# Attention and a selective scan in one kernel: the end, where only the scan is left, with its sums on TensorE two scans later and its side jobs moved once per scan

## The chip, the cores and the metric

The kernel runs on one core of one Trainium2 chip. A core has five engines with a queue each: TensorE (PE in the profile, its weight loads PEld), VectorE (DVE), ScalarE (ACT), GpSimd (POOL) and SyncE (SP), which here issues nearly all transfers between memory and the chip's on-chip memory. The metric is the time of one execution on the device in microseconds; lower is better. The time shown is the median of three runs.

## The reference, cut to what matters

Layer 0 is attention over 4 images of 64 x 64 pixels, each 4096 tokens of 128 channels, with 4 heads, and a layer norm. Layer 1 adds three things that it computes from that: a 3 x 3 convolution, a mixing in the frequency domain, and a Mamba block. The Mamba block is what this change is about. Its core is a scan with 256 inner channels and 16 states for each:

```python
def step(h, inp):
    xt, dtt, Bt, Ct = inp
    dA = jnp.exp(dtt[..., None] * A)
    h = dA * h + dtt[..., None] * Bt[:, None, :] * xt[..., None]
    y = jnp.einsum('bdn,bn->bd', h, Ct)
    return (h, y)
...
return ys.transpose(1, 0, 2) + x * D
...
y = y * jax.nn.silu(z)
return jnp.einsum('bld,od->blo', y, out_proj_w)
```

So for each of the 16 states there is a decay dA, an input term dt·B·x, a recurrence along the tokens, and a product with C; the 16 products and x·D are summed, multiplied by the gate silu(z), and projected.

## The kernel before, in words

The 4 x 4096 tokens are cut into 32 chunks of 512 (eight to an image). 128 channels lie on the 128 partitions, and the 512 tokens of a chunk along a row. The 256 inner channels are two halves.

The order of all work is written out by hand as a loop over steps `t` (the loop at the end of the function). Attention takes one step per block of 128 keys for one pair of heads and one chunk of queries: 64 steps a chunk, up to step 2048. In each step TensorE computes scores twice (L450 for the row maxima, L490 for the exponentials), VectorE takes maxima (L457), ScalarE takes exponentials (L498), and TensorE multiplies with the values (L510).

The scan runs beside it, 144 steps later, so that it goes on for 2.2 chunks after attention has ended, up to step 2190. One scan (one state of one half) is two steps; a chunk has 32 scans. At an odd step the next scan is prepared: `scan_decay` puts dA into a bank of PSUM with ScalarE (L823), `scan_input_term` forms the input term `db` (L828, GpSimd during attention, VectorE after it), and `scan_load` brings the rows of B and C, spread over all partitions, with a DMA from SP's queue (L806, or L812 for one that goes into memory that the keys and values of attention have left). At an even step `scan_state` runs the recurrence on VectorE (L839), copies the last value of the state (L848) and multiplies with C on GpSimd (L849), and adds the product to the sum. Which engine adds depends on the chunk: up to chunk 29 GpSimd (L866 the first time, with x·D, and L868), for the chunks 30 and 31 TensorE, which multiplies with the identity and sums in PSUM (L861, L862). In these two chunks the scan's result `hs` goes into one of four tiles that held values of attention (`VA[v % 4]`, V in the profile), otherwise into one of two buffers.

Everything else of layer 1 and the small steps of attention are jobs: Python generators that `Plan.step` moves on. A job yields a string of what its next stretch needs: P, D or A for a place on TensorE, VectorE or ScalarE, B for a bank of PSUM (there are two), x and f for buffers, or nothing. `Plan.step` sorts the jobs by rank and gives each whose need is met one stretch, and goes on at once with a job only if it needs P alone. How many places there are is told at each step. After attention it is called at every step, that is twice per scan, with four places for each of the three engines:

```python
if t < -LEAD or t > HALVES * NT:
    plan.step(t, {"D": 4, "P": 4, "A": 4})
```

The instructions of a step are put in the engines' queues in the order in which the program issues them, and each queue is worked off in that order. Within one odd step the decay, the input term and the load come first, then the jobs; within an even step the scan, its product and its sum come first.

The jobs that still run after attention are: `normalise` (the last one: L537 to L554, with four small DMAs and VectorE's reciprocal L545) and `output_projection` (L569 to L606) of chunk 31, `mamba_input` (L648 to L669), `scan_input` (L683 to L708), with the sigmoid (L622 to L632: Abs, Exp, Ln on ScalarE, a difference on VectorE, Exp), `scan_bc` (L720 to L730), `scan_dt` (L738 to L770) and `spectral` (L878 to L900) of chunk 31; `convolve` (L913 to L923) and `gate` (L779 to L787) of the chunks 30 and 31; `scan_output` (L934 to L985) of the chunks 29 to 31, which multiplies the sums with the gates (L957 or L960), projects them (L970), adds (L976, L943, L944) and stores; and the four `flips` of the last image. `scan_output` of a chunk is due two steps after the chunk's 64 steps of scanning.

Of the kernel before, what the change touches and what calls it, by code (L numbers as in the profile page):

```python
# [9 lines left out]
F32 = mybir.dt.float32  # L10
F32R = mybir.dt.float32r
AF = mybir.ActivationFunctionType
ALU = mybir.AluOpType
# [4 lines left out]
P = 128  # L18
# [5 lines left out]
L = 512  # L24
# [3 lines left out]
NH = DI // P  # L28
NS = 16
# [54 lines left out]
class Job:  # L84
# [17 lines left out]
class Plan:  # L102


    def __init__(self, banks, buffers):
        self.t = None
        self.places = buffers
        self.seq = 0
        self.later = []
        self.jobs = []  # L110
        self.free = list(range(banks))
        self.freed = []
# [11 lines left out]
    def step(self, t, places):  # L124

        self.t = t
        self.places |= places
        self.free += [bank for when, bank in self.freed if when <= t]
        self.freed = [e for e in self.freed if e[0] > t]
        for e in sorted((e for e in self.later if e[0] <= t), key=lambda e: e[:3]):  # L130
            self.jobs.append((e[1], e[0], e[2], Job(e[3])))
            self.later.remove(e)
        self.jobs = sorted((j for j in self.jobs if not j[3].done), key=lambda j: j[:3])
        kept = 0
        for *_, job in self.jobs:
            bank = None
            if "B" in job.need and len(self.free) <= kept:
                continue
            if any(c != "B" and not self.places[c] for c in job.need):
                kept += "B" in job.need  # L140
                continue
            for c in job.need:
                if c == "B":
                    bank = self.free.pop(0)
                else:
                    self.places[c] -= 1
            job.advance(bank)
            while not job.done and job.need == "P" and self.places["P"]:
                self.places["P"] -= 1
                job.advance(None)  # L150
        self.jobs = [j for j in self.jobs if not j[3].done]

# [5 lines left out]
def attention_then_conv_mamba(  # L158
# [17 lines left out]
    nc = tc.nc  # L176
# [3 lines left out]
    NT = N // P  # L180
    CHUNKS = B * NCH
    HALVES = CHUNKS * PAIRS
# [19 lines left out]
    for h in range(HEADS):  # L202
        k, j = divmod(h, 2)
        c = COL["bk"] + k
# [8 lines left out]
    for h in range(HEADS):  # L213
        k, j = divmod(h, 2)
        c = COL["bq"] + h
# [38 lines left out]
    ident = cst[:, K_ID : K_ID + P]  # L254
# [68 lines left out]
    plan = Plan(2, {"x": 2, "f": 1})  # L323
# [311 lines left out]
    xps, xss, dts, us, accs, gates, xds, bcds = ({} for _ in range(8))  # L635
# [194 lines left out]
    def scan_state(c, v):  # L830

        n, hf = divmod(v, NH)
        k = hf * NS + n
        assert (c, hf) in scaled
        if c >= CHUNKS - 2:
            hs = flat(VA[v % 4])
        else:
            hs = loc.tile([P, L], F32, tag="hs", name=f"hs_{c}_{k}")
        nc.vector.tensor_tensor_scan(  # L839
            hs,  # L840
            dA.pop((c, v)),
            db.pop((c, v)),
            state[:, k : k + 1] if c % NCH else zero,
            ALU.mult,
            ALU.add,
        )
        if c % NCH < NCH - 1:
            nc.gpsimd.tensor_copy(state[:, k : k + 1], hs[:, L - 1 :])  # L848
        nc.gpsimd.tensor_tensor(hs, hs, bcs[c, n][1], ALU.mult)  # L849
        if hf == NH - 1 and (c, n) in taken:  # L850
            spare.append((plan.t + 6, taken.pop((c, n))))
        elif hf == NH - 1:
            ring[0] += 1
        if c >= CHUNKS - 2:

            if v == 0:
                late = psum.tile([P, NH, L], F32, tag=f"s{CHUNKS - c}", name=f"acc_{c}")
                for h in range(NH):
                    accs[c, h] = late[:, h, :]
            if n == 0:  # L860
                nc.tensor.matmul(accs[c, hf], ident, xss[c][hf], start=True, stop=False)  # L861
            nc.tensor.matmul(accs[c, hf], ident, hs, start=False, stop=n == NS - 1)  # L862
        elif n == 0:
            acc = loc.tile([P, L], F32, tag=f"acc{hf}", name=f"acc_{c}_{hf}")
            accs[c, hf] = acc
            nc.gpsimd.tensor_tensor(acc, xss[c][hf], hs, ALU.add)  # L866
        else:
            nc.gpsimd.tensor_tensor(accs[c, hf], accs[c, hf], hs, ALU.add)  # L868

    hxs, yms, edges, wd, ymd = {}, {}, set(), {}, {}  # L870

# [74 lines left out]
    def scan_output(c):  # L946

        b, i = divmod(c, NCH)
        late = i < NCH // 2
        yield "f"  # L950
        while not all(gates[c]) or c not in yms:
            yield ""

        for hf in range(NH):
            if c >= CHUNKS - 2:
                acc = loc.tile([P, L], F32, tag=f"acc{hf}", name=f"acc_{c}_{hf}")
                nc.vector.tensor_tensor(acc, accs[c, hf], gates[c][hf], ALU.mult)  # L957
                accs[c, hf] = acc
            else:
                nc.gpsimd.tensor_tensor(accs[c, hf], accs[c, hf], gates[c][hf], ALU.mult)  # L960
        if not late:
            wr = load_flipped(c)
        for _ in range(3):
            yield ""
        bank = yield "PB"
        pf = bank_tile(bank, [P, L], f"py1_{c}")
        for hf in range(NH):
            if hf:
                yield "P"
            nc.tensor.matmul(  # L970
                pf, outw[:, hf, :], accs[c, hf], start=hf == 0, stop=hf == NH - 1
            )
        yield "D"
        plan.release(bank, 2)
        ob = loc.tile([P, L], F32, tag="ob", name=f"ob_{c}", bufs=1)
        nc.vector.tensor_tensor(ob, yms.pop(c), pf, ALU.add)  # L976
        if late:
            yield ""
            ymd[c] = dram.tile([P, L], F32, tag="ymd", name=f"ymd_{c}", bufs=NCH)
            nc.sync.dma_start(ymd[c], ob)  # L980
        else:
            add_flipped(ob, wr)
            yield ""
            yield ""
            nc.sync.dma_start(out[b, :, i * L : (i + 1) * L], ob)  # L985
        plan.places["f"] += 1
# [20 lines left out]
    LEAD = 7  # L1007
    SLOT = PAIRS * NT
    LAG = 2 * SLOT + 16
# [19 lines left out]
    for c in range(CHUNKS):  # L1029
        t0 = (c + 1) * SLOT  # L1030
        plan.at(t0, 0, load_residual(c))
        plan.at(t0 + 16, 1, mamba_input(c))
        plan.at(t0 + SLOT + 30, 3, convolve(c))
        plan.at(c * SLOT + LAG + 6, 3, gate(c))
        plan.at((c + 1) * SLOT + LAG + 2, 0, scan_output(c))
    for b in range(B):
        for i in range(NCH // 2):
            plan.at((b + 1) * NCH * SLOT + 44 + 10 * i, 4, flips(b * NCH + NCH // 2 - 1 - i))
# [1 line left out]
    t = 6 - SLOT  # L1040
    loaded = 0
    end = (CHUNKS + 3) * SLOT
    while t < end or not plan.idle():
        H, m = divmod(t, NT)
        if 0 <= H < HALVES:
            scores_for_exp(H, m)
        h1, s1 = divmod(t + LEAD, NT)
        if 0 <= h1 + 1 < HALVES:
            scores_for_max(h1 + 1, s1)
        H, m = divmod(t - 1, NT)  # L1050
        last = m == NT - 1
        if last and 0 <= H < HALVES:
            times_values(H, m)
        c, s = divmod(t - LAG, SLOT)
        odd = s % 2 == 1
        if -1 <= c < CHUNKS:
            v = c * STATES + s // 2
            if not odd:
                if v >= 0:
                    scan_state(*divmod(v, STATES))  # L1060
            else:
                if 0 <= v + 1 < CHUNKS * STATES:
                    scan_decay(*divmod(v + 1, STATES))
                if 0 <= v + 2 < CHUNKS * STATES:
                    late = t > HALVES * NT
                    scan_input_term(
                        *divmod(v + 2, STATES), nc.vector if late else nc.gpsimd
                    )

                if loaded < CHUNKS * NS and loaded // NS in bcds:  # L1070
                    if ring[0] or spare[0][0] <= t:
                        scan_load(*divmod(loaded, NS))
                        loaded += 1
        if t < -LEAD or t > HALVES * NT:
            plan.step(t, {"D": 4, "P": 4, "A": 4})
        elif odd:
            plan.step(t, {"D": 2, "P": 2, "A": 2})
        else:
            plan.step(t, {"D": 0, "P": 0, "A": 1})
        if not last and 0 <= H < HALVES:  # L1080
            times_values(H, m)
        t += 1
# [76 lines left out]
```

## Time and profile before

| what | value |
| --- | --- |
| median of three runs | 6060.06 us (6060.05 to 6060.12) |
| the profiled execution's own time | 6062.53 us |
| its span | 6060.8 us |
| TensorE busy | 5849.3 us, 97% |
| VectorE busy | 4360.3 us, 72% |
| ScalarE busy | 3585.5 us, 59% |
| GpSimd busy | 4488.8 us, 74% |
| last instruction of attention's values ends, scan 12 of chunk 29 begins | 5820 us |
| first scan of chunk 30 begins | 5851.66 us |
| first scan of chunk 31 begins | 5970.70 us |
| last scan ends | 6050.2 us |

The profile is one execution, and its times count from the start of its span. A row of a timeline gives start, duration, engine, line, operation and operands (out<-in), and in brackets how long the engine had been idle just before and what ended that. A row of waits names the waiting engine and line, whom it waited for, the total in us, the number of times and the longest. A row of the windows gives for a stretch of the span the busy time of each engine with the number of its instructions, then TensorE's granted clock as a share of full speed, the DMA engines' share and GB/s. A float32 matmul stands there as two records.

Two names differ in the profile from the text: the tiles V and K are also what the scan uses after attention, for its states and for B and C. A busy TensorE row is modelled at its end, so it is not TensorE at its best.

### The profile page before, as it was taken

The numbers are of one execution on the slowest core, as the hardware profiler recorded it, in microseconds if no ns is written. First come the engines' busy times: TensorE is split into PE (matmuls) and PEld (weight loads), VectorE is DVE, ScalarE is ACT, GpSimd is POOL, SyncE is SP. The second block draws the span as 40 slices with busy tenths as digits, with TensorE's granted clock in tenths as the row PEclk, the third lists the DMA queues.
The fourth block names the chain that finished last, engine by engine and source line by source line (L and its number), as shares of the span: only waits on it lengthen the run. The fifth ranks groups of instructions, "written<-read, shape, count | busy, mean of one in ns | idle before, by whom it ended". The sixth has DMA issues, their size and how long they took to land. (4 is left out here: it accounts for less than half of the span.)

```text
span 6060.8 us, 82716 instructions
## 1 busy us (share of the span) xinstructions
PE 5849.3 (97%) x31370; PEld 2443.2 (40%) x31370; DVE 4360.3 (72%) x4565; ACT 3585.5 (59%) x4826; POOL 4488.8 (74%) x4530
## 2 busy tenths in 40 slices
PE   5999999999999999999999999999999999999966
PEld 2444444444444444444444444444444444444322
DVE  4557777777777777777777777777777777777647
ACT  1455666666666666666666666666666666666643
POOL 0006888778887777888887888877888887788877
PEclk7999999999999999999999999999999999999988
DMA  4012222224333322223432222222433222222233
GB/s 124 25 36 58 66 72 75 69 73 109 86 84 76 73 67 74 76 64 87 105 89 78 73 66 71 75 71 70 110 81 84 70 69 64 66 67 63 71 86 84
DMA packets 266641, 455.28 MB, mean 75 GB/s; under 512 B 46688, under 2 KB 48256, under 8 KB 266240
## 3 DMA queue, kind: packets, MB, share of 16 engines
q1 hardware_dynamic: 261584, 448.11, 28.3%
q8 instruction: 246, 4.03, 0.3%
q10 hardware_dynamic: 4656, 1.87, 0.1%
q14 instruction: 155, 1.27, 0.1%
HBM read 375.68 MB, written 65.80 MB: 73 GB/s over the span
## 5 line engine op out<-in xcount | busy, mean ns | idle before, releaser
L457 DVE TENSOR_REDUCE part<-s 128x2 f32<-128x1024 f32 x2048 | 2499.2, 1221 | 1413.1 <-PE s L450 1409.3
L498 ACT ACTIVATE e<-s 128x1024 f32<-128x1024 f32 x2048 | 2095.6, 1023 | 2121.3 <-PE s L490 2116.7
L510 PE MATMUL po<-e,V 128*33 128x512 f32 x8192 | 2180.9, 605 | 2.4 <-DVE oz L521 0.3
L490 PE MATMUL s<-Q,K 64*128 64x512 f32 x8192 | 1500.6, 444 | 13.5 <-ACT e L498 10.2
L450 PE MATMUL s<-K,Q 64*128 64x512 f32 x8192 | 1314.7, 399 | 38.0 <-DVE part L457 28.9
L849 POOL TENSOR_TENSOR hs<-hs,bc 128x512 f32<-128x512 f32 x952 | 1215.9, 1277 | 170.7 <-DVE hs L839 101.4
L490 PEld LDWEIGHTS s<-Q,K 64*128 64x128 f32 x8192 | 610.2, 184 | 1736.3 <-ACT e L498 1237.8
L828 POOL TENSOR_TENSOR db<-u,bc 128x512 f32<-128x512 f32 x948 | 1215.9, 1283 | 0.0
L868 POOL TENSOR_TENSOR acc<-acc,hs 128x512 f32<-128x512 f32 x900 | 1154.7, 1283 | 70.6
L839 DVE TENSOR_TENSOR_SCAN hs<-dA,state,db 128x512 f32<-128x512 f32 x832 | 1060.6, 1275 | 52.6 <-ACT dA L823 37.9
L450 PEld LDWEIGHTS s<-K,Q 64*128 64x128 f32 x8192 | 752.9, 186 | 295.3 <-DVE part L457 128.1
L490 PE MATMUL s<-MX,sel 64*128 64x512 f32 x4096 | 808.3, 391 | 0.0
L823 ACT ACTIVATE dA<-dt,negA 128x512 f32<-128x512 f32 x1024 | 703.4, 687 | 113.4 <-DVE V L839 54.7
L848 POOL COPY state<-hs 128x1 f32<-128x1 f32 x864 | 159.0, 184 | 789.4 <-DVE hs L839 785.7
L510 PEld LDWEIGHTS po<-e,V 128*33 128x33 f32 x8192 | 305.3, 109 | 886.6 <-issue 840.9
L490 PEld LDWEIGHTS s<-MX,sel 64*128 64x128 f32 x4096 | 383.5, 185 | 90.8
L913 PE MATMUL pf<-xp,cw 128*128 128x512 f32 x576 | 287.9, 618 | 0.0
L554 POOL TENSOR_TENSOR op<-op,rz 128x512 f32<-128x512 f32 x32 | 40.9, 1278 | 178.5 <-DMA rz<-rd 175.6
L839 DVE TENSOR_TENSOR_SCAN hs<-dA,zero,db 128x512 f32<-128x512 f32 x128 | 163.2, 1275 | 1.0 <-POOL db L828 0.7
L862 PE MATMUL acc<-V,cst 128*128 128x512 f32 x128 | 89.1, 798 | 74.3 <-POOL V L849 74.0
L913 PEld LDWEIGHTS pf<-xp,cw 128*128 128x128 f32 x576 | 96.6, 188 | 118.5 <-issue 117.0
L708 POOL TENSOR_TENSOR xs<-xs,sg_x 128x512 f32<-128x512 f32 x64 | 82.3, 1286 | 76.5 <-ACT sg_x L632 76.5
(146 smaller groups left out, 3555.2 us busy)
## 6 DMA issues: line engine op xcount, KB each, us to landing
bc<-bcd SPq DMA_DIRECT2D x487, 512.0 KB
Q<-qd SPq DMA_DIRECT2D x256, 128.0 KB
K<-kd SPq DMA_DIRECT2D x64, 256.0 KB
K<-bcd SPq DMA_DIRECT2D x42, 256.0 KB
vd<-vst SPq DMA_DIRECT2D x32, 264.0 KB
V<-vd SPq DMA_DIRECT2D x32, 264.0 KB
xq<-in_x SPq DMA_DIRECT2D x32, 256.0 KB
xk<-in_x SPq DMA_DIRECT2D x32, 256.0 KB
```

The source lines that it names most:

```text
L450: nc.tensor.matmul(sc[:, j, :], QT[H][rows[j], n, t * P : (t + 1) * P], KK[k][m][rows[j], :], start=n == 0, stop=n == 1,)
L457: nc.vector.tensor_reduce(part[H][:, t, :, m], sc, AX.X, ALU.max)
L490: nc.tensor.matmul(s[:, j, :], sel[rows[j], :] if n == 2 else KK[k][i][rows[j], t * P : (t + 1) * P], mov[rows[j], :], start=n == 0, stop= ...
L498: nc.scalar.activation(e, s, AF.Exp)
L510: nc.tensor.matmul(po[H][used[j], :], VA[i][:, t, 2 * k + j, :], e[:, j, :], start=m == 0, stop=m == NT - 1,)
L823: nc.scalar.activation(dA[c, v], dts[c][hf], AF.Exp, scale=negA[:, k : k + 1])
L828: engine.tensor_tensor(db[c, v], us[c][hf], bcs[c, n][0], ALU.mult)
L839: nc.vector.tensor_tensor_scan(hs, dA.pop((c, v)), db.pop((c, v)), state[:, k : k + 1] if c % NCH else zero, ALU.mult, ALU.add,)
L848: nc.gpsimd.tensor_copy(state[:, k : k + 1], hs[:, L - 1 :])
L849: nc.gpsimd.tensor_tensor(hs, hs, bcs[c, n][1], ALU.mult)
L868: nc.gpsimd.tensor_tensor(accs[c, hf], accs[c, hf], hs, ALU.add)
L913: nc.tensor.matmul(pf, cw[:, k, :], xps[c][:, dy : dy + RPC, dx : dx + W], start=k == 0, stop=False)
```

## The change

There are four parts, all of them for the steps after attention.

1. `late` in `scan_state` no longer goes by the chunk (30 and 31) but by the step, so that the last six scans of chunk 29 also write into the four V tiles and are summed by TensorE.
2. The sums are not issued with the product. They are put on a list with a due step four later, and `add_states`, called at each step after attention's end ahead of the jobs, issues those that are due. Four steps are two scans.
3. Jobs are moved on only at odd steps, once per scan, with four places for VectorE and TensorE and six for ScalarE, and a job goes on within the step as long as it needs one place of P, A or D alone and there is one.
4. Chunk 29 has two partial sums for each half, GpSimd's and TensorE's. Its output joins them with an addition on VectorE and multiplies with the gate there too, as chunks 30 and 31 did before. The output of the chunks 29, 30 and 31 is due six steps after the chunk's 64 steps instead of two.

The bank for TensorE's sum is named by the chunk's parity, and the loop guards against an empty list of spare places. The diff, cut:

```diff
-            while not job.done and job.need == "P" and self.places["P"]:
-                self.places["P"] -= 1
+
+            while not job.done and job.need in ("PAD" if self.late else "P"):
+                if not job.need or not self.places[job.need]:
+                    break
+                self.places[job.need] -= 1
                 job.advance(None)
...
-        if c >= CHUNKS - 2:
+        late = plan.t > HALVES * NT + 1
+        if late:
             hs = flat(VA[v % 4])
...
-        if c >= CHUNKS - 2:
-
-            if v == 0:
-                late = psum.tile([P, NH, L], F32, tag=f"s{CHUNKS - c}", name=f"acc_{c}")
-                for h in range(NH):
-                    accs[c, h] = late[:, h, :]
-            if n == 0:
-                nc.tensor.matmul(accs[c, hf], ident, xss[c][hf], start=True, stop=False)
-            nc.tensor.matmul(accs[c, hf], ident, hs, start=False, stop=n == NS - 1)
+        if late:
+
+            if c not in sums_late:
+                sums_late[c] = psum.tile(
+                    [P, NH, L], F32, tag=f"s{1 + c % 2}", name=f"acc_{c}"
+                )
+            terms = [hs] if n else [xss[c][hf], hs]
+            for x in terms:
+                waiting.append((plan.t + 4, c, hf, x, n == NS - 1 and x is hs))
...
+    def add_states():
+        while waiting and waiting[0][0] <= plan.t:
+            _, c, hf, x, last = waiting.pop(0)
+            nc.tensor.matmul(
+                sums_late[c][:, hf, :], ident, x, start=(c, hf) not in begun, stop=last
+            )
+            begun.add((c, hf))
...
-            if c >= CHUNKS - 2:
-                acc = loc.tile([P, L], F32, tag=f"acc{hf}", name=f"acc_{c}_{hf}")
-                nc.vector.tensor_tensor(acc, accs[c, hf], gates[c][hf], ALU.mult)
-                accs[c, hf] = acc
+            if c in sums_late:
+                total = sums_late[c][:, hf, :]
+                if (c, hf) in accs:
+                    nc.vector.tensor_tensor(accs[c, hf], accs[c, hf], total, ALU.add)
+                    total = accs[c, hf]
+                else:
+                    accs[c, hf] = loc.tile([P, L], F32, tag=f"acc{hf}", name=f"acc_{c}_{hf}")
+                nc.vector.tensor_tensor(accs[c, hf], total, gates[c][hf], ALU.mult)
...
-        plan.at((c + 1) * SLOT + LAG + 2, 0, scan_output(c))
+        plan.at((c + 1) * SLOT + LAG + (2 if c < CHUNKS - 3 else 6), 0, scan_output(c))
...
-        if t < -LEAD or t > HALVES * NT:
+        plan.late = t > HALVES * NT
+        if plan.late:
+            add_states()
+            if odd:
+                plan.step(t, {"D": 4, "P": 4, "A": 6})
+            plan.t = t
+        elif t < -LEAD:
             plan.step(t, {"D": 4, "P": 4, "A": 4})
```

In the built program this leaves every engine's order as it was up to the end of attention, and after it GpSimd has eight instructions fewer, VectorE four more, and SP the same transfers, some of them in another order.

More of the change, by code (lines that the diff above doesn't have):

```diff
@@ L106, in __init__ @@
         self.t = None
+        self.late = False
         self.places = buffers
@@ L868, in scan_state @@
             nc.gpsimd.tensor_tensor(accs[c, hf], accs[c, hf], hs, ALU.add)
+    sums_late, waiting, begun = {}, [], set()
+    def add_states():
[5 more added lines that the diff above has]
+            begun.add((c, hf))
     hxs, yms, edges, wd, ymd = {}, {}, set(), {}, {}
@@ L1070, in attention_then_conv_mamba @@
                 if loaded < CHUNKS * NS and loaded // NS in bcds:
-                    if ring[0] or spare[0][0] <= t:
+                    if ring[0] or spare and spare[0][0] <= t:
                         scan_load(*divmod(loaded, NS))
                         loaded += 1
-        if t < -LEAD or t > HALVES * NT:
+        plan.late = t > HALVES * NT
[5 more added lines that the diff above has]
+        elif t < -LEAD:
             plan.step(t, {"D": 4, "P": 4, "A": 4})
```

## The prediction

> **What bounds the kernel now.** I read the 40 slices first: TensorE is at 9 tenths to the 38th slice and falls to 6 after it, so almost the whole span is attention and only the end is anything else. In the built order no instruction of any engine moves before the end of attention, so 5820 us of the 6060.8 us span cannot change. Next I cut the rest by chunk of the scan with the windows table. The last eight scans of chunk 29 run to 5852, chunk 30 to 5971, chunk 31 to 6050, and then comes the end of the last output.
>
> ```profile
> core 0: us, PE busy (x) PEld busy (x) DVE busy (x) ACT busy (x) POOL busy (x), PEclk, DMA share, GB/s
> 5820.00:5852.00 32.00, 6.25 (x12) 2.04 (x10) 20.97 (x31) 9.30 (x16) 28.66 (x29) 0.60 0.20 54
> 5852.00:5971.00 119.00, 72.48 (x118) 26.53 (x118) 82.28 (x85) 45.91 (x80) 79.25 (x91) 0.72 0.50 139
> 5971.00:6050.00 79.00, 52.74 (x96) 17.25 (x94) 63.89 (x67) 26.72 (x41) 58.83 (x39) 0.91 0.20 47
> 6050.00:6061.00 11.00, 4.33 (x9) 1.27 (x8) 2.17 (x4) 0.00 (x0) 3.01 (x4) 0.90 0.06 24
> ```
>
> Only the first stretch has a nearly full engine (POOL, 28.66 of 32.00). In the other two nobody is full, and VectorE, which carries every scan, is idle for 36.7 and 15.1 us. With 11.0 in the first stretch that is 62.8 us of idle VectorE; nothing longer can be won there. The rows without side jobs show what a scan costs when nothing disturbs it: 1.92 us from scan to scan, 1.28 for the scan and the rest for its input term.
>
> ```profile
> 6034.29 1.28 DVE L839 TENSOR_TENSOR_SCAN V<-dA,state,db 128x512 f32<-128x512 f32 x1
> 6035.60 0.69 DVE L828 TENSOR_TENSOR db<-u,K 128x512 f32<-128x512 f32 x1
> 6036.22 1.28 DVE L839 TENSOR_TENSOR_SCAN V<-dA,state,db 128x512 f32<-128x512 f32 x1
> ```
>
> Then the waits from 5820 on: who waited, for whom, us in total, times, longest.
>
> ```profile
> PE acc L862 <- POOL V L849: 74.0, 39, 6.1
> DVE V L839 <- ACT dA L823: 19.6, 8, 5.4
> DVE ob L976 <- PE py L970: 12.5, 3, 6.9
> DVE hs L839 <- POOL acc L868: 10.6, 5, 4.0
> DVE sg_z L630 <- ACT ln_z L627: 6.9, 1, 6.9
> DVE conv L693 <- ACT xi L688: 4.2, 1, 4.2
> ```
>
> TensorE, hardly loaded, sits 74 us waiting for GpSimd's product, because the sum of a state is put in its queue right after the state's product was issued. Whatever a side job asks of TensorE stands behind that wait. The timeline shows the longest case.
>
> ```profile
> 5862.74 1.26 POOL L849 TENSOR_TENSOR V<-V,bc 128x512 f32<-128x512 f32 x1
> ...
> 5864.06 0.45 PEld L862 LDWEIGHTS acc<-V,cst 128*128 128x128 f32 x2 [3.38 <-POOL V L849]
> ...
> 5867.57 1.88 PE L970 MATMUL py<-acc,outw 128*128 128x512 f32 x4
> ...
> 5869.49 0.69 DVE L976 TENSOR_TENSOR ob<-ym,py 128x512 f32<-128x512 f32 x1 [6.87 <-PE py L970]
> 5870.10 1.28 DVE L839 TENSOR_TENSOR_SCAN V<-dA,state,db 128x512 f32<-128x512 f32 x1
> ```
>
> GpSimd's products let the sums go at 5864.06, the output product follows them, and VectorE, whose next instruction needs it, starts the next scan at 5870.10 after 6.87 us of nothing.
>
> **What the Trainium skill says.** *TensorE: Matmul & The Clock Gate*, "Architectural detail", says that ScalarE's, VectorE's and GpSimd's queues are strict FIFOs, while TensorE can pull weight loads ahead; the stall just shown agrees for matmuls and VectorE. The same page, "What's actually happening", says that TensorE runs at half rate after an idle window of about 3.4 us and at full rate after a busy one: the trace agrees, one state's sum takes 1.12 us in dense stretches and 2.08 us after long waits. *SBUF — State Buffer*, "Who interferes with whom", says that a VectorE tensor_tensor with both inputs in SBUF and a GpSimd instruction exclude each other; agreed, the input term takes 0.69 us alone and up to 1.79 us here.
>
> **The change, part by part.**
> *Sums two scans later.* In chunks 30 and 31 these idle stretches before VectorE's instructions lead back to TensorE behind a product: 6.87 (py), 4.20 (pi), 2.11 (p1), 3.35 (pw), 2.58 (pd) in chunk 30, 4.05 (py) and 3.31 (pz) in chunk 31, together 26.5 us. Two scans later (3.8 us) the product, 1.27 us, is usually done, and TensorE goes through. What is late next is ScalarE's chain of the job, below. A tile is written again four scans later, so a sum has two scans to spare.
> *Chunk 29's last states.* Six sums leave GpSimd (6 x 1.44 = 8.7 us) and two gate products (2 x 1.49 = 3.0). VectorE gets four instructions, two joins and two gates, 0.65 each as L957's pair in 1.29: 2.6 us, in chunk 30's stretch and in VectorE's own sequence, so paid. TensorE gets six sums of at most 2.08 us where it is busy 6.25 of 32 us: nothing, unless it is late for the fifth scan. The scans no longer wait for two hs buffers: 10.6 us of idle go. Two things come in their place. The load of the reciprocals' input (L542) now stands in SP's queue behind the load of chunk 30's first B and C, which waits for a product that ended at 5831.7; before it was issued at 5822.39. It lands some 4 us after 5832.2 (rd to rz took 4.1), and VectorE's reciprocal stands ahead of scan 14, so VectorE stops at about 31.4 and goes on at 36: 4.6 us. Then rd and rz (4.1 and some 3) bring GpSimd's L554 to 43.7, the projection (2.07) to 47.1, and VectorE, ready at 43.9, waits 3.3 us at L572 ahead of chunk 30's first scan. 10.6 go, 7.9 come, and the L630 that stands earlier costs nothing new: about 3.5 us won with the small gaps.
> *Jobs once per scan, chains in one step.* A sigmoid now puts Abs and Exp into one step and Ln into the next: 0.62 + 0.62 + dA 0.69 + Ln 0.68 is 2.6 us, up to 3.9 with the copy 0.60 and two edge copies, while VectorE has one scan and one input term, 1.92, before it meets L630. So each leaves 1 to 2 us: 2.1, 1.8 and 1.4 in chunk 30 (the first hides behind join and layer norm), 1.8 twice in chunk 31. The projection pd stands behind four taps of the convolution (0.88 each, 16 records in 7.03) and a sum: 1.8. The convolution's result ym stands ahead of the next decay on ScalarE: six taps and a sum, 6.2 us, less 2.7 of VectorE's work: 3.7 in chunk 30. In chunk 31 ten taps and two sums, 10.6, less 7: 4. The dt chain of the first half ahead of decay 9: 1.8. GpSimd gets both halves' L761 to L763 (2 x 4.6) and a flip (1.9) close together, scans then outrun the four tiles: 4 and another 2. Loads for the flips now have two scans to land instead of one; I keep 2 us for the one at the start of chunk 31.
> *Sum of what stays.* Chunk 30: 2.1 + 1.8 + 1.4 + 1.8 + 3.7 + 1.8 + 6 = 18.6; the terms' waits for GpSimd, which are inside the 82.28 us of busy time, cover part of it, I take 16. Its length: 82.3 + 2.6 + 16 = 101 instead of 119, won 18. Chunk 31: 63.9 + 3.6 + 4 + 2 and 1.5 for the outputs' products = 75 instead of 79, won 4. The end keeps its 11 us, as its order is the same. In all 3.5 + 18 + 4 = 25.5 us. The profiled execution took 6062.53 with a span of 6060.8; the runs' median 6060.06 is 0.7 below the span. 6060.8 - 25.5 - 0.7 = 6034.6, so **6035**.
> *Bounds.* The residual waits are the unknown, no row shows them. Nothing less than none: 62.8 - 2.6 = 60 us won, 6000. At the other end all 62.8 come back in new places, with 2.6 us more: 6063, and more only by the last rival.
>
> **Rivals.**
> *VectorE is nearly full.* For it: TensorE, ScalarE and GpSimd have 46, 73 and 40 us to spare in chunk 30. Against it: the chains above have only one scan to hide in. With a third of my 35 us of residual waits (7.9 + 16 + 11), 23 more are won: 6012.
> *Products more than two scans late.* GpSimd is busy 79.25 of 119 us, and without the two gates 76 in 101 is 75%; if bursts keep it two scans behind for most of chunk 30, TensorE blocks as before and that chunk keeps its idle time. Then 3.5 + 4 are won: 6053, no change as measured.
> *ScalarE's answer in VectorE's queue, slower.* Seven sigmoids (one in chunk 29, four in 30, two in 31) have L630 ahead of a scan. If ScalarE starts each only after a half-rate input product (2.1) behind two half-rate sums (4.2), the wait is 2.6 + 6.3 = 8.9 each without cover: 62 us, with 7.7 for the two ym, 7.9 in chunk 29 and 2.6 new work 80 against 62.8 won: 6078. It costs more than is won from 6.4 us per sigmoid. Against it: only one of the seven showed as much before (6.9).
> *It does not do what it says:* excluded, the built order has the sums two scans later.
>
> **How the numbers follow.** Forecast, 6022 to 6047: 0.62. VectorE nearly full, 6000 to 6022: 0.17. Late products, 6048 to 6072: 0.14. Slower: 0.07. A measurement of this kernel tells about 0.2%, 12 us, from no change, so faster is 0.79, same 0.14, slower 0.07. The range 6012 to 6053 leaves out half of the second and third case and the last.
>
> **What would show it.** The same rows: TensorE waiting for the product well under 74 us; L976 after py, L693 after xi near nothing; the hs wait gone and a wait of VectorE at the reciprocal and at L572; new waits of the sigmoid's difference for Ln of 1 to 2 us; ym ahead of a decay still 3 to 4. Chunk lengths near 28, 101 and 75. I am wrong if chunk 30 stays above 110, if attention's part moves, or if VectorE's input terms slow far beyond their 0.9 us.

## The result and the profile after

The changed kernel takes 6039.84 us (median of 7 runs, 6038.33 to 6043.57) where the kernel before takes 6060.05 (7 runs beside it): ratio 0.9968, 95% interval 0.9957 to 0.998, 20.2 us less. The profiled execution took 6038.33 with a span of 6036.5. The lines have moved: the scan is L844 (before L839), its product L854 (L849), the sum on TensorE L880 (L862), the decay L827 (L823), the sigmoid's difference L634 (L630) after Ln L631 (L627), the addition to the projection L995 (L976), the reciprocal L549 (L545), the attention projection's result L576 (L572).

The windows table of the kernel after, cut as that of before (the columns are the same: PE, PEld, DVE, ACT, POOL busy, then clock, DMA share, GB/s):

```profile
5818.00:5846.00 28.00, 8.99 (x14) 2.73 (x13) 19.01 (x21) 9.77 (x15) 23.64 (x24) 0.68 0.28 63
5846.00:5953.00 107.00, 70.73 (x126) 25.51 (x125) 84.20 (x98) 46.33 (x80) 76.61 (x87) 0.74 0.51 153
5953.00:6026.00 73.00, 53.69 (x97) 17.80 (x95) 64.69 (x68) 26.90 (x41) 60.45 (x39) 0.90 0.19 51
6026.00:6037.00 11.00, 4.24 (x8) 1.27 (x8) 2.00 (x4) 0.00 (x0) 2.84 (x4) 0.97 0.07 25
```

VectorE's busy column hardly changes; it is the lengths that shrink. Measured from scan to scan in the timeline (from the first scan after attention, eight scans before the end of chunk 29, to the first scan of chunk 30, from there to the first scan of chunk 31, and on to the end of the last scan), the three stretches of time took 30.8, 119.0 and 79.5 us before and 27.5, 106.9 and 73.0 after. So 3.3 + 12.1 + 6.5 = 21.9 us were won there. Attention ended 2.2 us earlier in this execution, and the end stayed (10.6 before, 10.5 after). VectorE's idle time in the windows fell from 11.0 + 36.7 + 15.1 to 9.0 + 22.8 + 8.3 us.

The waits of VectorE after the end of attention, and from the whole list of waits the row of TensorE:

```profile
PE acc L880 <- POOL V L854: 63.5, 38, 14.9
```

```profile
DVE V L844 <- ACT dA L827: 10.4, 3, 5.1
DVE V L844 <- PE acc L880: 8.3, 2, 5.0
DVE oz L525 <- ACT oz L524: 7.3, 1, 7.3
DVE zc L549 <- DMA zc<-zd: 6.3, 1, 6.3
DVE dtr L731 <- ACT dtr L730: 3.7, 1, 3.7
DVE sg_x L634 <- ACT ln_x L631: 2.8, 2, 1.5
```

TensorE still waits for products, but less than the 63.5 suggests: 14.9 of it is the first sum of chunk 29, in a stretch where it holds up nobody. What matters is who stands behind. `hs` waiting for GpSimd (10.6 before) and `conv` waiting for `xi` (4.2) are gone from the list, `ob` waiting for `py` fell from 12.5 to 2.5. What is left are answers of ScalarE (dA 10.4 us after 19.6, Ln 2.8 and 2.3 after 6.9, dtr 3.7 after 2.6) and, twice, a sum that frees a tile (8.3 after 3.8); the small DMA (zc) is new. The oz row is the wait for attention's last values, ahead of the three stretches; it was 7.3 us before too. The case shown of before, the output of chunk 29, in the timeline after:

```profile
5866.54 1.12 PE L880 MATMUL acc<-V,cst 128*128 128x512 f32 x2 [0.33 <-POOL V L854]
...
5867.50 1.91 PE L989 MATMUL py<-acc,outw 128*128 128x512 f32 x4
...
5871.51 0.68 DVE L995 TENSOR_TENSOR ob<-ym,py 128x512 f32<-128x512 f32 x1
```

Before, the matmul of the sum stood like this (the 3.38 us in the prediction's view are those of its weight load):

```profile
5864.06 3.68 PE L862 MATMUL acc<-V,cst 128*128 128x512 f32 x4 [2.50 <-POOL V L849]
```

Now it waits 0.33 us instead of 2.50, the output product follows it, and VectorE meets its addition with no idle time at all (no bracket), where it had stood still for 6.87 us.

What now holds VectorE up longest in chunk 30 is another chain, near its end (timeline after):

```profile
5941.69 0.32 SPq L1012 DMA_DIRECT2D ob<-ymd  x1
...
5945.18 1.35 POOL L958 TENSOR_TENSOR ob<-ob,wr 128x504 f32<-128x504 f32 x1 [4.40 <-DMA wr<-wd]
...
5948.22 7.61 PE L880 MATMUL acc<-V,cst 128*128 128x512 f32 x10 [6.26 <-POOL V L854]
...
5950.40 1.28 DVE L844 TENSOR_TENSOR_SCAN V<-dA,state,db 128x512 f32<-128x512 f32 x1 [4.98 <-PE acc L880]
```

SP's load of a flip could be issued only at 5941.69, since it had waited 4.5 us for the store out of the one buffer `ob`. GpSimd, in order, stands 4.40 us at the flip's addition, with the scan's products behind it; the sums are late by as much, and the fifth scan finds its tile not yet read.

### The profile page after: what moved, and what is told of

It reads as the page before. It is cut to its first block, busy times and chain, and to the rows that moved or that the text cites. A ratio compares the mean times of both kernels' runs of the same rounds, so it can differ in the third digit from the quotient of the medians.

```text
span 6036.5 us, 82731 instructions
## 1 busy us (share of the span) xinstructions
PE 5847.1 (97%) x31382; PEld 2443.1 (40%) x31382; DVE 4360.0 (72%) x4569; ACT 3586.6 (59%) x4826; POOL 4482.6 (74%) x4522
## 3 DMA queue, kind: packets, MB, share of 16 engines
q14 instruction: 155, 1.27, 0.1%
## 5 line engine op out<-in xcount | busy, mean ns | idle before, releaser
L854 POOL TENSOR_TENSOR hs<-hs,bc 128x512 f32<-128x512 f32 x948 | 1211.0, 1277 | 170.3 <-DVE hs L844 101.3
L844 DVE TENSOR_TENSOR_SCAN hs<-dA,state,db 128x512 f32<-128x512 f32 x826 | 1052.8, 1275 | 41.9 <-ACT dA L827 40.1
L827 ACT ACTIVATE dA<-dt,negA 128x512 f32<-128x512 f32 x1024 | 703.2, 687 | 115.7 <-DVE V L844 69.5
L844 DVE TENSOR_TENSOR_SCAN hs<-dA,zero,db 128x512 f32<-128x512 f32 x128 | 163.2, 1275 | 0.9 <-POOL db L832 0.7
L880 PE MATMUL acc<-V,cst 128*128 128x512 f32 x140 | 95.0, 783 | 63.6 <-POOL V L854 63.5
```

What stands on the lines that cost most here:

```text
L827: nc.scalar.activation(dA[c, v], dts[c][hf], AF.Exp, scale=negA[:, k : k + 1])
L844: nc.vector.tensor_tensor_scan(hs, dA.pop((c, v)), db.pop((c, v)), state[:, k : k + 1] if c % NCH else zero, ALU.mult, ALU.add,)
```

## The experiments

Four questions: which of the parts wins the time, which costs some, whether the waits that stay can be taken away one by one, and whether there is a better version. The ratios are against runs of the kernel before on the same chip, whose medians were 6059.58, 6063.29 and 6060.06 us in the three groups below. Single stretches of time come from one profiled execution each. For orientation, the three of each kernel, in us, beside the medians. "Later" for the sums means due four steps after the state; the outputs of the chunks 29 to 31 are due four steps later than before in every row but the first.

| kernel | jobs' rhythm | chunk 29's last states summed by | sums | stretches | median |
| --- | --- | --- | --- | --- | --- |
| before | before | GpSimd | at once | 30.8 / 119.0 / 79.5 | 6060.05 |
| after | changed | TensorE | later | 27.5 / 106.9 / 73.0 | 6039.84 |
| sums_at_once | changed | TensorE | at once | 31.3 / 140.8 / 89.4 | 6090.99 |
| jobs_as_before | before | TensorE | later | 29.9 / 101.6 / 68.9 | 6033.66 |
| chunk29_gpsimd | changed | GpSimd | later | 33.5 / 106.8 / 72.4 | 6045.26 |
| delay_only | before | GpSimd | later | 30.8 / 102.2 / 68.9 | 6032.47 |
| delay_one_scan | before | GpSimd | two steps later | 30.8 / 104.6 / 73.5 | 6040.61 |
| chains_twice | chains, each step | TensorE | later | 29.8 / 106.6 / 78.3 | 6045.85 |
| best_a | before | GpSimd | later | 30.8 / 101.3 / 67.5 | 6028.90 |
| best_b | before | TensorE | later | 29.5 / 97.2 / 68.5 | 6028.10 |

### The parts, taken apart

**sums_at_once.** The changed kernel, its sums due at once:

```diff
-                waiting.append((plan.t + 4, c, hf, x, n == NS - 1 and x is hs))
+                waiting.append((plan.t, c, hf, x, n == NS - 1 and x is hs))
```

Expected: 

> The changed kernel, but each state's sum is issued with its product again instead of two scans later; chunk 29's last states and the jobs stay as changed. If the delay of the sums is what wins (my theory), TensorE waits for GpSimd's product ahead of the jobs' matmuls again, and most of the gain goes: 6052 to 6056 us, with idle time of VectorE before the adding of py, before the convolution taps after pi and before dtr. If the jobs' new rhythm wins (rival), it stays at 6040 to 6043.

Measured: 6090.99 us (6090.3 to 6092.36), ratio 1.0052, interval 1.0038 to 1.0065. It is slower than the kernel before, by 31 us, and far above what I had expected; that the other parts matter little without the delay was wrong. From the changed kernel it differs in the delay alone, and by 51 us. VectorE's waits in it:

```profile
DVE sg_z L634 <- ACT ln_z L631: 20.1, 4, 7.6
DVE V L844 <- ACT dA L827: 18.5, 3, 7.8
DVE ob L995 <- PE py L989: 14.8, 3, 7.0
```

The longest of the first row, in the timeline:

```profile
5875.05 1.26 POOL L854 TENSOR_TENSOR V<-V,K 128x512 f32<-128x512 f32 x1
...
5876.37 2.07 PE L880 MATMUL acc<-V,cst 128*128 128x512 f32 x2 [6.38 <-POOL V L854]
...
5878.24 1.91 PE L783 MATMUL pz<-xp,inw 128*128 128x512 f32 x2
...
5880.19 0.60 ACT L789 ACTIVATE zg<-pz 128x512 f32<-128x512 f32 x1 [6.56 <-PE pz L783]
...
5884.42 0.69 DVE L634 SCALAR_TENSOR_TENSOR sg_z<-zg,ln_z 128x512 f32<-128x512 f32 x1 [7.56 <-ACT ln_z L631]
```

Product, sum, input projection, ScalarE's copy, Abs, Exp and Ln, and only then VectorE's difference, ahead of the next scan: a serial loop through four engines. This is the mechanism of the prediction's slower rival, TensorE's sums ahead of a sigmoid whose answer stands in VectorE's queue. It is real; the delay of the sums is what keeps it from happening in the changed kernel.

**jobs_as_before.** The changed kernel with the old way of moving jobs:

```diff
-            while not job.done and job.need in ("PAD" if self.late else "P"):
+            while not job.done and job.need in "P":
...
-            if odd:
-                plan.step(t, {"D": 4, "P": 4, "A": 6})
-            plan.t = t
+            plan.step(t, {"D": 4, "P": 4, "A": 4})
```

Expected: 

> The changed kernel, but jobs advance twice per scan with four places each and go on within a step only for TensorE, as before; sums two scans later and chunk 29's states as changed. If the delay wins, 6036 to 6045: the answers of ScalarE are asked for with less time, but VectorE meets them later. If the jobs' rhythm wins, 6052 to 6058.

Measured: 6033.66 us (6031.09 to 6034.18), ratio 0.9956, interval 0.9943 to 0.9968. That is below both ranges: the delay keeps its gain without the new rhythm, and the old rhythm is some 6 us better than the changed one. In the list of VectorE's waits the difference's wait for Ln is absent; dA (10.1 us in six waits, the longest 3.8), xr (7.2) and dtr (5.6) lead it. In the timeline no sigmoid's difference has idle time of a microsecond ahead of it.

**chunk29_gpsimd.** The changed kernel with GpSimd summing all of chunk 29:

```diff
-        late = plan.t > HALVES * NT + 1
+        late = c >= CHUNKS - 2
```

Expected: 

> The changed kernel, but chunk 29 is summed by GpSimd to its end in two buffers, with its gates there too. My sum gave this part 3.5 us, and VectorE loses four instructions of 2.6 us: 6039 to 6044. If freeing GpSimd of these sums is what wins (rival), it goes back to 6050 or more.

Measured: 6045.26 us (6044.06 to 6046.3), ratio 0.9975, interval 0.9965 to 0.9985; some 5 us above the changed kernel and 1 above the range I had given, all of it in the first stretch (33.5 instead of 27.5).

**delay_only.** Both edits above together, so that only the delay of the sums is left of the change, and the later due time for the outputs of the chunks 29 to 31, which the delay needs:

```diff
-            while not job.done and job.need in ("PAD" if self.late else "P"):
+            while not job.done and job.need in "P":
...
-        late = plan.t > HALVES * NT + 1
+        late = c >= CHUNKS - 2
...
-            if odd:
-                plan.step(t, {"D": 4, "P": 4, "A": 6})
-            plan.t = t
+            plan.step(t, {"D": 4, "P": 4, "A": 4})
```

Expected: 

> The kernel before with one part alone: the sums of chunks 30 and 31 two scans later (and the outputs due four steps later, which that needs). If the delay wins alone, 6040 to 6047; if it needs the jobs' new rhythm or chunk 29's states, 6054 or more.

Measured: 6032.47 us (6031.78 to 6036.36), ratio 0.9956, interval 0.9944 to 0.9969: 27.1 us less than before, in chunk 30 16.8 and in chunk 31 10.6, nothing in the first stretch. I had expected 6040 at best. VectorE's waits:

```profile
DVE V L844 <- ACT dA L827: 12.0, 6, 3.8
DVE hs L844 <- POOL acc L873: 10.6, 5, 4.0
DVE dtr L731 <- ACT dtr L730: 5.6, 1, 5.6
```

The hs row of before is back unchanged, and still this kernel is faster than the changed one. So the delay, with the later outputs, brings more than the whole change; the jobs' new rhythm gives some of it back. Where GpSimd sums chunk 29, the two rhythms stand side by side in this one group and differ by 12.8 us (chunk29_gpsimd 6045.26, delay_only 6032.47). Chunk 29's states on TensorE win about 5 us in the new rhythm (6045.26 to 6039.84) and nothing that can be told in the old (6032.47 against 6033.66): there the wait for hs (10.6 us) only becomes the wait for xr (7.2).

The later outputs are a second edit in delay_only, and they move other jobs: before, the projection pd (5903.20) stood ahead of the taps of chunk 30's convolution (eight in a row from 5906.42), and here seven taps (from 5887.04) stand ahead of pd (5894.00). The kernel before with the later outputs alone was not run, so their share of the 27.1 us is open. Where only the delay differs, in sums_at_once against the changed kernel, its effect, in the new rhythm, does not depend on them.

### The size of the delay, and the waits one by one

**delay_one_scan.** delay_only with half the delay in steps:

```diff
-                waiting.append((plan.t + 4, c, hf, x, n == NS - 1 and x is hs))
+                waiting.append((plan.t + 2, c, hf, x, n == NS - 1 and x is hs))
```

`plan.t` still holds the step before, both when the state is put on the list and when the list is read, so the sum is issued four steps after its state with 4, and two steps after it, one scan, with 2. The jobs' matmuls of as many steps go ahead of it.

Expected: 

> The kernel before with the sums of chunks 30 and 31 one scan later instead of two (which alone gave 6032.5). If what counts is that the product is ready when TensorE meets its sum, one scan (1.92 us against a product of 1.27 and GpSimd's own backlog) is not always enough: 6037 to 6046. If it is only that the jobs' matmuls stand ahead of the sum in the queue (rival), one scan is as good: 6031 to 6035.

Measured: 6040.61 us (6038.4 to 6044.54), ratio 0.9965, interval 0.9952 to 0.9979. With the shorter delay it is 22.7 us below its runs of before, with the longer one 27.1 below its own; the two ratios' intervals overlap, so the 4 to 5 us between them, in chunk 31 above all (73.5 against 68.9), are likely and not certain. The time is in the first of the two ranges; still, letting the jobs' matmuls of two steps go ahead of the sum is most of the effect.

**zc_first.** The changed kernel, in which the load of the last reciprocals' input is issued one stretch of its job earlier, ahead of the load of B and C that waits for a product:

```diff
-        yield ""
+        if H < HALVES - 1:
+            yield ""
         zc = att.tile([P, 2 * L // P], F32, tag="zc", name=f"zc_{H}")
```

Expected: 

> The changed kernel, but the load of the reciprocals' input is issued together with the store it reads, ahead of chunk 30's first B and C on SP. Gone is VectorE's wait of 6.3 us at the reciprocal, and the output product comes earlier. If that wait is on the path: 6032 to 6036. If GpSimd, which gets to scan 13's product only at 5832.8, is late anyway (rival), the scans then wait for the four tiles and it stays at 6038 to 6041.

Measured: 6036.36 us (6033.14 to 6037.62), ratio 0.9955, interval 0.9943 to 0.9968. The wait of 6.3 us at the reciprocal is gone. Further on a scan waits 3.35 us for a tile, where none waited before, since the sums had to wait for GpSimd's products (its lines are one further on):

```profile
5837.42 5.49 PE L881 MATMUL acc<-V,cst 128*128 128x512 f32 x6 [15.89 <-POOL V L855]
5839.60 1.28 DVE L845 TENSOR_TENSOR_SCAN V<-dA,state,db 128x512 f32<-128x512 f32 x1 [3.35 <-PE acc L881]
5844.68 0.75 DVE L577 SCALAR_TENSOR_TENSOR xr<-pa,bo,xr 128x512 f32<-128x512 f32 x1 [2.34 <-PE pa L574]
```

The first stretch of time took 27.7 us, as with the wait (27.5). What this execution won lies in the chunks 30 and 31 (103.8 and 71.9 us instead of 106.9 and 73.0).

**ym_later.** The changed kernel, in which the convolution's result comes three stretches of its job, that is three scans, later, so that its products are done when ScalarE meets it ahead of a decay:

```diff
+        for _ in range(3 if plan.late else 0):
+            yield ""
         yield "A"
         plan.release(bank)
```

Expected: 

> The changed kernel, but ScalarE is given the convolution's result three scans later, so that it no longer stands ahead of the next decay. In the changed kernel VectorE waits 3.6 us in chunk 30 and 5.1 in chunk 31 there. If these are waits for ScalarE's order: both go, 6031 to 6034. If the sums that stand behind the ten taps on TensorE are what is late (rival), VectorE waits for the tiles instead: 6037 or more.

Measured: 6036.04 us (6034.2 to 6036.56), ratio 0.9955, interval 0.9942 to 0.9967. The two waits behind ym, 3.62 and 5.13 us, are gone; at the same places stand

```profile
5907.94 1.28 DVE L844 TENSOR_TENSOR_SCAN V<-dA,state,db 128x512 f32<-128x512 f32 x1 [1.30 <-PE acc L880]
5987.24 1.28 DVE L844 TENSOR_TENSOR_SCAN V<-dA,state,db 128x512 f32<-128x512 f32 x1 [2.28 <-PE acc L880]
```

Chunk 30 took 106.6 us (106.9), chunk 31 71.2 (73.0). GpSimd is not what was late here. Ahead of the first of these waits it had stood idle itself, and the sums ran with no idle time of TensorE, right behind the convolution's taps:

```profile
5904.04 0.71 POOL L853 COPY state<-V 128x1 f32<-128x1 f32 x1 [4.32 <-DVE V L844]
5904.24 1.88 PE L928 MATMUL pf<-xp,cw 128*128 128x512 f32 x4
5905.96 1.02 PE L933 MATMUL pf<-hx,g 128*128 128x512 f32 x2
5906.82 1.88 PE L880 MATMUL acc<-V,cst 128*128 128x512 f32 x4
```

This is the rival of the expectation, the sums behind the taps, with a smaller loss than it gave.

**flips_later.** The changed kernel; the last image's flips start ten steps earlier, with one stretch more between load and addition and one less before the store:

```diff
-        yield ""
-        yield ""
+        for _ in range(3 if plan.late else 2):
+            yield ""
         add_flipped(ob, wr)
-        yield ""
-        yield ""
+        for _ in range(1 if plan.late else 2):
+            yield ""
...
-            plan.at((b + 1) * NCH * SLOT + 44 + 10 * i, 4, flips(b * NCH + NCH // 2 - 1 - i))
+            plan.at((b + 1) * NCH * SLOT + (34 if b == B - 1 else 44) + 10 * i, 4, flips(b * NCH + NCH // 2 - 1 - i))
```

Expected: 

> The changed kernel, but the four flips begin five scans earlier and add three scans after their load was issued instead of two. GpSimd's wait of 4.4 us for the flipped rows, and behind it VectorE's 5.0 us for a sum, should go: 6033 to 6037, and the spread of 5 us between runs should narrow if it comes from that transfer. If the transfer is late because the store before it has not ended (rival), the wait stays: 6038 to 6042.

Measured: 6035.84 us (6034.21 to 6037.45), ratio 0.9955, interval 0.9942 to 0.9967. GpSimd's wait for the flipped rows fell from 4.40 to 1.95 us and did not go. VectorE's wait of 4.98 us became one of 3.36 for the same cause, a sum behind GpSimd's products; chunk 30 took 104.4.

In all three the wait that is taken away comes back in part as a wait for a tile whose sum is late: behind GpSimd's products in zc_first and flips_later, behind the convolution's taps on TensorE in ym_later. Their medians are 3 to 4 us under the changed kernel's, but its own runs here spread over 5, and it was not in that group; the ratios' intervals overlap.

### Where the jobs' rhythm loses, and a better version

**chains_twice.** The changed kernel, jobs called at every step, the chains within a step kept:

```diff
-            if odd:
-                plan.step(t, {"D": 4, "P": 4, "A": 6})
-            plan.t = t
+            plan.step(t, {"D": 4, "P": 4, "A": 4})
```

Expected: 

> The changed kernel with one thing changed: jobs are moved on at every step, so twice per scan as before the change, but a job still goes on within a step through places of P, A or D alone. Theory A: what costs 6 us in the changed kernel against the version with the old rhythm (6033.7) is the chains, which put a job's ScalarE work into one step and its VectorE answer only one scan behind. Then this stays at the changed kernel's time or above it, 6038 to 6046, with the sigmoid's waits for Ln as long as now. Theory B: the cost is the calling once per scan, which puts two stretches' worth of jobs into the same place ahead of a scan. Then it falls to 6031 to 6035, with waits like the old rhythm's (no wait for Ln, decay, dtr and the residual terms only).

Measured: 6045.85 us (6042.36 to 6049.14), ratio 0.9974, interval 0.9965 to 0.9984. Theory A holds, and with a larger number than it gave: against jobs_as_before (6033.66, in another group) only the chains differ, and they cost some 12 us. VectorE's waits:

```profile
DVE V L844 <- ACT dA L827: 12.6, 6, 8.3
DVE sg_z L634 <- ACT ln_z L631: 11.6, 5, 5.1
```

The longest wait for Ln, at 5905.51, starts at ScalarE's Abs:

```profile
5902.93 0.63 ACT L626 ACTIVATE sg_z<-zg 128x512 f32<-128x512 f32 x1 [3.67 <-POOL zg L791]
```

With chains the second half's sigmoid is queued so early that its one buffer `sg_z` is still to be read by GpSimd's gate product, and ScalarE, VectorE and the scan stand behind that. The sigmoids are not all of the cost. The longest wait of this kernel is that of a decay in chunk 31, which stands on ScalarE behind the convolution's result ym (begun at 5991.73):

```profile
5993.04 1.28 DVE L844 TENSOR_TENSOR_SCAN V<-dA,state,db 128x512 f32<-128x512 f32 x1 [8.29 <-ACT dA L827]
```

In jobs_as_before this wait was 2.39 us. Calling once per scan takes some 6 us of the chains' cost away (6039.4 in the same group, under after_again); why, was not varied by itself. Once per scan without chains was not tried.

**best_a** and **best_b.** delay_only and jobs_as_before, with three moves:

```diff
-        for _ in range(3):
+        for _ in range(9 if plan.late else 3):
...
-        yield ""
-        yield ""
+        for _ in range(5 if plan.late else 2):
+            yield ""
         add_flipped(ob, wr)
-        yield ""
-        yield ""
+        for _ in range(1 if plan.late else 2):
+            yield ""
...
-        plan.at(t0 + SLOT + 30, 3, convolve(c))
+        plan.at(t0 + SLOT + (52 if c == CHUNKS - 2 else 30), 3, convolve(c))
...
-            plan.at((b + 1) * NCH * SLOT + 44 + 10 * i, 4, flips(b * NCH + NCH // 2 - 1 - i))
+            plan.at((b + 1) * NCH * SLOT + (34 if b == B - 1 else 44) + 10 * i, 4, flips(b * NCH + NCH // 2 - 1 - i))
```

Expected of best_a: 

> The version that so far is fastest (old rhythm of the jobs, chunk 29 summed by GpSimd, only the sums two scans later; 6032.5) with three waits taken away by later or earlier starts: the convolution of chunk 30 starts 22 steps later so that the dt projection does not stand behind its taps (dtr, 5.6 us), the scaling of x ahead of a decay comes six stretches later (3.8 us), and the last image's flips start ten steps earlier with more room between load and addition (3.8 us). Theory A: these waits are what is left to win, 6 to 10 us of the 13 come off, 6022 to 6027. Theory B: GpSimd's backlog fills whatever is opened, as in the three single removals on the changed kernel (2 to 4 us each at most): 6029 to 6033, and a wait for the tiles behind GpSimd's products grows.

Expected of best_b: 

> The same three moves on the version that has the last states of chunk 29 on TensorE as well, with the old rhythm of the jobs (6033.7). Chunk 29's stretch took 32.5 us there and 33.7 with GpSimd's sums, so by both theories this is within 2 us of the version with GpSimd's sums: by theory A 6022 to 6028, by theory B 6029 to 6034.

Measured: best_a 6028.9 us (6028.28 to 6030.93), ratio 0.9947, interval 0.9934 to 0.9959; best_b 6028.1 us (6027.34 to 6028.99), ratio 0.9945, interval 0.9932 to 0.9957. Both are the fastest of the study; they lie between the two theories, best_b at the outer edge of A; the wait for a tile that B would have grow did not (3.4 us in all in either kernel, after 3.8 and 4.2). The three waits aimed at, in best_b's timeline:

```profile
5894.16 0.73 DVE L731 SCALAR_TENSOR_TENSOR dtr<-dtr,cst,pd 32x512 fp32r<-32x512 f32 x1 [3.52 <-ACT dtr L730]
5922.48 1.28 DVE L844 TENSOR_TENSOR_SCAN V<-dA,state,db 128x512 f32<-128x512 f32 x1 [5.78 <-ACT dA L827]
5944.57 1.28 DVE L844 TENSOR_TENSOR_SCAN V<-dA,state,db 128x512 f32<-128x512 f32 x1 [1.69 <-PE acc L880]
```

In jobs_as_before they were 5.59, 3.83 and 3.78. The middle one grew and changed its cause: the later convolution now puts ym ahead of that decay.

**after_again.** The changed kernel itself, in this last group.

Expected: 

> The changed kernel as it is, on the same chip as the three others, since its own runs so far spread from 6038.3 to 6043.6. If the 6 us between it and the old rhythm's version are real, it is at 6037 to 6043, slower than each of the others with a gap larger than both intervals; if they came from another chip or moment, it is within 2 us of the version with chains and two calls.

Measured: 6039.4 us (6037.21 to 6040.36), ratio 0.9962, interval 0.995 to 0.9975; stretches 27.3, 106.9 and 73.1. So its time is no accident of one chip, and on the same chip chains_twice lies above it and the two best versions about 11 us below, their slowest run under its fastest.

## Why the prediction was right, point by point

The forecast of 6035 was 4.8 us too low, with the sign, the mechanism and the order of size right. In part the parts' errors cancel: measured from scan to scan, chunk 29 won 3.3 us (3.5 forecast), chunk 30 12.1 (18) and chunk 31 6.5 (4). Step by step:

- *Nothing moves before the end of attention.* Right: the stretches begin at 5820.8 before and at 5818.7 and 5817.6 in two executions after, the scatter of single executions.
- *26.5 us of VectorE's idle time lead back to TensorE behind a product.* Right in the mechanism, and shown by sums_at_once and delay_only. In the changed kernel most of the rows named are gone or small: L995 after py 0 and 0.98 us (6.87 and 4.05), xi and p1 no row of a microsecond; only pd grew. That delay_only won just 27.1 us is in part chance: 16.8 and 10.6 in the two chunks where the rows named add to 19.1 and 7.4. There dtr's wait grew from 2.58 to 5.59 and a decay waits 3.03 us at a new place, while the sigmoid's wait of 6.91 is gone, which the sum had left out (before, ScalarE had waited 6.18 us there for pdt, which stood on TensorE behind the convolution's taps).
- *Chunk 29: 10.6 go, 4.6 and 3.3 come, 3.5 won.* The sum came out right (3.3), its terms less so. The reciprocal cost 6.28 instead of 4.6, xr 2.41 instead of 3.3. That the reciprocal's wait is the cost was too simple: zc_first took it away, and the tiles' wait took its place. And the gain hangs on the jobs' rhythm: some 5 us in the new, none in the old.
- *New work of VectorE, 2.6 us.* Joins and gates show at 0.67 to 0.69 us with one of 1.44; chunk 30's busy time rose by 1.9.
- *What stays in chunk 30: 18.6, taken 16; length 101.* This is the step that was off most: 22.8 us stayed idle, length 106.9. The single waits were 1.31, 1.50 and 1.27 for the sigmoids (2.1, 1.8, 1.4), 3.62 for ym (3.7), 1.63 for the decay after it (1.8 for the dt chain): near enough. The projection pd, at dtr, took 3.65 instead of 1.8. GpSimd's backlog took 3.36 and 4.98 instead of 4 and 2, the second through the flip's load, which I had seen but put into chunk 31 at 2 us. That is 21.3 in sum, and taking 16 from 18.6 because the terms' busy time would cover some of it was wrong: the busy time (84.2 against 82.3 + 2.6) gave back less than 1 us.
- *Chunk 31: waits of 11 and 75 long.* 1.01, 0.98 and 5.13 us showed, 73.0 long; one of the two sigmoids waited for nothing, and the flip came earlier.
- *The end keeps its 11 us.* Right, 10.5.
- *Jobs once per scan* were priced by their residual waits alone, and the text did not ask what the delay would give with the jobs left alone. Its own numbers pointed there: the 26.5 us are whole in the two chunks, and of the waits that stay, those at the sigmoids come from the chains.

Of the rivals, *VectorE nearly full* is not what happened, since idle time of about 40 us is left in the three stretches. *Products more than two scans late* did happen, in two places of chunk 30 (3.36 and 4.98), not for most of it. *Slower* did not, but sums_at_once shows its mechanism: 27.0 us at six sigmoids, 20.1 and 6.9, which is 4.5 each where the rival took 8.9, and 6090.99 us in all.

What stays open: the share of the later outputs in what delay_only won; that a late sum takes back what a removed wait gives was read from the timelines and not varied by itself; and the three single removals were not run beside the changed kernel.

## What to carry to other kernels

In an engine that works in order, an instruction that waits for a slow partner should be issued when the partner is done, behind whatever else the engine has to give to others; here this edit, with the later outputs that it needs, was worth 27 us, more than the whole change. Issuing the stretches of a job close together brought, in these runs, the instruction that waits for an answer closer to the one that asks, and cost some 12 us: keep a scan or two of other work between a question to another engine and the instruction that needs its answer. Before adding a further edit to one that works, run the one alone; and take away single waits only with an eye on the engine that is next behind, since part of the time came back there in each of the three cases tried.

## What the runs showed of the hardware that was not expected

TensorE's granted clock in the chunks 30 and 31 was 0.72 and 0.91 before and 0.77 and 0.98 with the delay alone, with the same number of matmul records in it (117 and 96) and less busy time (72.2 and 53.2 us before, 66.3 and 48.5 then, cut from scan to scan): the same matmuls, closer together, ran faster. With the jobs' new rhythm the clock hardly rose: 0.74 and 0.90 in the changed kernel, against 0.80 and 0.98 in jobs_as_before, so a part of what separates the rhythms may be the clock. That a denser TensorE has the higher clock agrees with what the prediction drew from the Trainium skill, *TensorE: Matmul & The Clock Gate*, "What's actually happening", on idle windows. I had counted only the waits, and TensorE's 10 us less of busy time in the two chunks are a part of the gain that I did not separate.

Executions of the changed kernel spread more than I had thought: 6038.3 to 6043.6 in one group, 6037.2 to 6040.4 in another, while the kernel before kept within 0.9 us beside the first and within 6.7 beside the second. I have no cause for it. Differences of 2 or 3 us between groups mean nothing here.
